# Two attention layers: column totals of two groups moved from TensorE to VectorE, and two chunks of statistics from VectorE to ScalarE

## The chip, the cores and the metric

The kernel runs on one core of one Trainium2 chip. The metric is device time in microseconds (us), lower is better; several runs are timed, and one further execution is recorded by the hardware profiler. The engines are called by the profile's letters: PE is TensorE (PEld its weight loads), DVE is VectorE, ACT is ScalarE, POOL is GpSimd, SP is SyncE, which here only issues transfers. Each engine works through its own instructions in order, and waits for the others by semaphores.

## The reference

The input `x` is eight images of 512 channels by 32x32 positions, all fp32. Two attention layers follow each other, each added to its input. Layer 0, which the change concerns, is cut here to what matters; `_gn` is a group norm over 16 channels and all positions:

```python
x = x + _L0_conv_ref(_gn(x), ...)          # layer 0
x = x + _L1_conv_ref(_gn(x), ...)          # layer 1

def _L0_conv_ref(x, gn_w, gn_b, qkv_w, qkv_b, proj_w, proj_b):
    normed = groupnorm(x) * gn_w + gn_b
    q, k, v = split(einsum('oc,bct->bot', qkv_w, normed) + qkv_b, 3)
    # 8 heads of 64 channels, 1024 positions each
    weight = softmax(einsum('bct,bcs->bts', q * scale, k * scale))   # over s
    a = einsum('bts,bcs->bct', weight, v)
    return einsum('oc,bct->bot', proj_w, xf + a) + proj_b
```

So per image and head, layer 0 needs the exponentials of 1024x1024 scores, their sums over one axis (the softmax denominators), the weighted values, and a division. Layer 1 begins with the group norm of layer 0's result, for which each channel's mean and variance over its 1024 positions are needed.

## The kernel before

**Stages.** Layer 0 runs image after image ("batch" `b`, 0 to 7); after all of them layer 1 does the same. In a batch, `attention0(b, ag)` computes the attention of layer 0; then the projections `qk0` and `v0` of the next batch, and `out0(b)`, the output projection of this one, which adds into the tiles `xs[b][c]` (four chunks of 128 channels by 1024 positions) and stores them to device memory (line 1080). At the last batch the projections of layer 1's first image stand in the place of the next batch's.

**The attention.** It goes over 64 steps `i`. Eight steps make a group `g` (two heads, 512 query positions, eight blocks of 128 key positions). A step has: four matmuls of scores into a PSUM tile `s` (line 1102; two such tiles), one ScalarE exponential of 128x1024 into a tile `e` (line 1107; seven such tiles, pool `epool`), one VectorE addition of `e` into the group's accumulator `zacc` (lines 1115 and 1117), and four matmuls of values (line 1130). When a group is complete, ScalarE copies its result out of PSUM to `u` (line 1141), and three jobs follow: `totals(g)` sums `zacc` over its partitions, `reciprocals(g)` inverts the sums and sends them through device memory so that they come back broadcast over partitions in `rzb`, and `finish(g)` multiplies `u` by `rzb` and adds it to `xa` (lines 1203 and 1205).

`totals` has two forms. For odd groups TensorE multiplies `zacc` by ones (line 1149), ScalarE copies the row out of PSUM (line 1154), and one transfer on SP brings it to a column `zc`. For even groups VectorE transposes `zacc` in blocks of 32x32 and reduces along the rows, twice (lines 1162 and 1163), transposes the small result (line 1167), and four transfers on SP gather it; `reciprocals` then adds one reduce (line 1179).

**Order.** The order of instructions on all engines is the order in which the Python code issues them (`manual_schedule`). The loop takes two steps at a time: scores of `i` and `i+1`, then values and sums of `i-2` and `i-1`, then what an `Agenda` holds for the slots `i` and `i+1`. A group that ends at step `i-1` puts `totals` at slot `i+2`, `reciprocals` at `i+6` (TensorE form) or `i+8` (VectorE form), and `finish` at `i+12`. Work with fixed slots in the same agenda:

- `start_xa` (line 886), four ScalarE passes that begin the tile `xa`, at slots 2, 4, 6, 8;
- `stats_out(b - 1, c)`, the statistics of the previous batch's output chunk `c` by two `bn_stats` and one `bn_aggr` on VectorE (lines 664 and 665), at slots 4, 7, 12, 15, and one slot after each the load of the next batch's chunk into the tile that this frees;
- `stats0(b + 1)`: the next batch's norm, from slot 18 on. ScalarE makes two passes over each chunk (lines 838 and 844), VectorE a chain of small operations whose last part, `scale` (lines 812 to 825), stands at slot 49; two tiny matmuls stand between;
- `normalize0(b + 1, c)` (line 880), ScalarE's normalisation of the next batch, at slots 51, 54, 57, 60;
- in batches 0 to 2, four VectorE operations that combine weights, at slots 13, 14, 16, 17 (lines 784 to 790).

After the loop, `combine_right` (lines 899 to 902) forms four operands `tmp` from the normalised tile on VectorE, in the buffers of `e`. TensorE's first two products of the next projection need only the normalised tile, the third needs the second of these operands (line 900).

Of the kernel before, what the change touches and what calls it, by code (L numbers as in the profile page):

```python
# [9 lines left out]
F32 = mybir.dt.float32  # L10
I32 = mybir.dt.int32
AF = mybir.ActivationFunctionType
# [6 lines left out]
P = 128  # L19
# [448 lines left out]
def tile_two_attention_layers(  # L468
# [19 lines left out]
    nc = tc.nc  # L488
# [224 lines left out]
    with ExitStack() as l0:  # L713
# [168 lines left out]
        def start_xa(b, c):  # L882
            if c == 0:
                xa_t[b] = act.tile([P, NCC, T], F32, tag="xa", name=f"xa_{b}")
            gs = st0[b]
            nc.scalar.activation(
                xa_t[b][:, c], xs[b][c], AF.Identity,
                bias=gs.nb[:, c : c + 1], scale=gs.r1[:, c : c + 1],
            )
# [194 lines left out]
        def stats_out(b, c):  # L1084
            channel_stats(stat, xs[b][c], mvs[:, b, c], f"o0_{b}_{c}")

        NG = NT
        NI = NFB * (H // 2) * NG

        def attention0(b, agenda):  # L1090
# [51 lines left out]

            def totals(g):

                if g % 2:
                    HB = FB // 2
                    z = ps_a.tile([P, FB], F32, tag="a0", name=f"z_{b}_{g}", bufs=2)[:, :HB]
                    for c in range(4):
                        nc.tensor.matmul(
                            z[c * 32 : c * 32 + 32], ones[:, :32], zacc[g][:, c // 2, ts(c % 2, HB)],  # L1150
                            start=True, stop=True, tile_position=(0, c * 32),
                        )
                    row = zpool.tile([P, HB], F32, tag="row", name=f"row0_{b}_{g}", bufs=1)
                    nc.scalar.copy(row, z)
                    zc[g] = stat.tile([P, T // P], F32, tag="zc", name=f"zc_{b}_{g}")
                    nc.sync.dma_start(out=zc[g], in_=row[0::32])
                    return
                HN = FB // 32
                pz = stat.tile([P, 2, HN], F32, tag="pz", name=f"pz_{b}_{g}")
                for m in range(2):  # L1160
                    zt = zpool.tile([P, FB], F32, tag="zt", name=f"zt_{b}_{g}_{m}", bufs=1)
                    nc.vector.transpose(zt, zacc[g][:, m])
                    nc.vector.reduce_sum(
                        pz[:, m], zt.rearrange("p (n i) -> p n i", i=32), axis=AX.X
                    )
                pt = stat.tile([P, 32], F32, tag="pt", name=f"pt_{b}_{g}")
                nc.vector.transpose(pt, pz.rearrange("p m n -> p (m n)"))
                zc[g] = stat.tile([32, 4, 32], F32, tag="zc4", name=f"zc_{b}_{g}")
                for c in range(4):
                    nc.sync.dma_start(out=zc[g][:, c], in_=pt[c * 32 : c * 32 + 32])  # L1170

            def reciprocals(g):

                nc.vector.tensor_add(u[g][0], u[g][0], u[g][1])
                R, W = (P, T // P) if g % 2 else (32, 32)
                zs = zc[g]
                if g % 2 == 0:
                    zs = stat.tile([32, 32], F32, tag="zs0", name=f"zs_{b}_{g}")
                    nc.vector.reduce_sum(zs, zc[g].rearrange("p c j -> p j c"), axis=AX.X)
                rz = stat.tile([P, 32], F32, tag="rz0", name=f"rz_{b}_{g}")[:R, :W]  # L1180
                nc.vector.reciprocal(rz, zs)
                zd = dram.tile([2, FB], F32, tag=f"zd0_{b}_{g}", name=f"zd0_{b}_{g}")
                nc.sync.dma_start(
                    out=zd if g % 2 else zd.rearrange("m (n j) -> (m n) j", j=32), in_=rz
                )
                rzb[g] = zpool.tile([P, FB], F32, tag="rzb", name=f"rzb_{b}_{g}")
                for m in range(2):
                    nc.sync.dma_start(
                        out=rzb[g][m * D : m * D + D], in_=zd[m].partition_broadcast(D)
                    )  # L1190
                col = b * H + g
                junk = stat.tile([P, 32], F32, tag="junk0", name=f"junkz_{b}_{g}")[:R, :W]
                nc.vector.tensor_scalar(
                    junk, zs, 1.0, 0.0, ALU.mult, ALU.add, accum_out=chk[:R, 1, col : col + 1]
                )
                nc.vector.scalar_tensor_tensor(
                    junk, rz, 1.0 / RZ_MAX, rz, ALU.mult, ALU.mult,
                    accum_out=chk[:R, 0, col : col + 1],
                )
# [5 lines left out]
                nc.vector.tensor_add(dst, dst, u[g][0])  # L1205


            for i in range(0, NI + 2, 2):
                if i < NI:
                    scores(i)  # L1210
                    scores(i + 1)
                if i >= 2:
                    for w in (i - 2, i - 1):
                        values(w)
                        sums(w)
                    if (i - 1) % NG == NG - 1:
                        g = (i - 1) // NG
                        agenda.at(i + 2, lambda g=g: totals(g))
                        agenda.at(i + 6 + 2 * (g % 2 == 0), lambda g=g: reciprocals(g))
                        agenda.at(i + 12, lambda g=g: finish(g))  # L1220
                agenda.run(i)
                agenda.run(i + 1)
# [19 lines left out]
        for b in range(B):  # L1242
# [1 line left out]
            ag = Agenda()  # L1244
            ag.at(1, lambda: bias_xa(b))
            for c in range(NCC):
                ag.at(2 + 2 * c, lambda c=c: start_xa(b, c))
            for c, slot in enumerate((4, 7, 12, 15)):
                if b > 0:
                    ag.at(slot, lambda c=c: stats_out(b - 1, c))  # L1250
                if more:
                    ag.at(slot + 1, lambda c=c: load_x(b + 1, c))
# [4 lines left out]
                for i, slot in enumerate((13, 14, 16, 17, 19)):  # L1257
                    ag.at(slot, lambda which=which, i=i: combine_left(which, [i]))
            if more:
                stats0(b + 1, ag, 18)  # L1260
                for c in range(NCC):
                    ag.at(51 + 3 * c, lambda c=c: normalize0(b + 1, c))
                ag.at(32, lambda: load_left("k", b + 1))
                ag.at(33, lambda: load_left("v", b + 1))
            else:

                def load_first():
                    t = n_t["1"] = shared.tile([P, NCC, T], F32, tag="n", name="y_0")
                    for c in range(NCC):
                        nc.sync.dma_start(out=t[:, c], in_=x1_d[0][ts(c, P), :])  # L1270

                ag.at(20, load_first)
                for slot, fn in zip((22, 25, 28), group_stages(0, B - 1, small_psum)):
                    ag.at(slot, fn)
                ag.at(32, lambda: load_left("q1", 0))
                ag.at(33, lambda: load_left("k1", 0))
                for c in range(NCC):
                    ag.at(49 + 4 * c, lambda c=c: normalize_to(n_t["1"][:, c], 0, c))
# [905 lines left out]
```

## Time and profile before

| What | Value |
|---|---|
| Median of 3 runs | 3907.03 us (3902.49 to 3908.03) |
| The profiled execution | 3899.99 us, its span 3898.1 us |
| Granted TensorE clock | 0.999 |
| TensorE matmul calls of totals (line 1149) | 32 calls, 256 records, 20.4 us busy |
| VectorE transposes and reduces of totals (lines 1162 and 1163) | 64 and 64, 708 and 686 ns each |
| VectorE statistics of the output (line 664) | 64, 680 ns each |
| ScalarE passes of the next batch's norm (lines 838 and 844) | 28 and 28, 1067 and 1156 ns each |

How to read the lines of the profile. A line of a group gives line number, engine, operation, the tile written, an arrow and the tiles read, shapes, how many, then busy time and the mean length of one in nanoseconds, then the time that the engine stood idle just before them and what it waited for. A timeline line gives start and length in us, the engine, the line number and the operation; lengths of merged rows can overlap the next start, since operations are pipelined, so the cost of one is read from start to start. The stretches give the busy time of each engine within each piece of the span. A matmul in fp32 appears as two records.

### The profile page before, as it was taken

How to read it: one execution, taken by the hardware profiler on the slowest of the kernel's cores; microseconds unless marked ns; L12 is line 12 of the kernel's file. 1: busy time of each engine (PE TensorE's matmuls, PEld its weight loads, DVE VectorE, ACT ScalarE, POOL GpSimd, SP SyncE). 2: the span in 40 equal slices, each digit the busy share in tenths (PEclk: the TensorE clock that was granted, in tenths of full speed). 3: DMA queues.
4: the chain of work that ended last, by engine and by line, in shares of the span. 5: the costliest groups of instructions: out<-in, count | busy, mean ns of one | idle time of the engine just before them, and what ended most of it. 6: DMA issues, size and time to landing. Idle time of an engine off the chain costs nothing. (4 is left out here: it accounts for less than half of the span.)

```text
span 3898.1 us, 95183 instructions
## 1 busy us (share of the span) xinstructions
PE 3845.0 (99%) x41612; PEld 1809.6 (46%) x41612; DVE 2840.8 (73%) x3921; ACT 1962.0 (50%) x2400; POOL 207.4 (5%) x210
## 2 busy tenths in 40 slices
PE   8999999999999999999999999999999999999999
PEld 4353535344353535344554544545545545445455
DVE  4858586675859485866967958859769668678598
ACT  1726354453627172534826717528438257176175
POOL 0000000000000000000110200201101102002000
PEclk9999999999999999999999999999999999999999
DMA  3313131111122121216947929749659479297385
GB/s 122 123 52 118 50 113 43 67 67 71 58 73 67 59 81 49 91 47 162 235 133 194 231 91 232 194 127 240 180 136 239 150 171 237 96 222 206 119 222 161
DMA packets 248440, 519.45 MB, mean 133 GB/s; under 512 B 49872, under 2 KB 57040, under 8 KB 241360
## 3 DMA queue, kind: packets, MB, share of 16 engines
q1 hardware_dynamic: 240832, 500.48, 45.3%
q0 software_dynamic: 7184, 12.81, 1.6%
q8 instruction: 328, 5.37, 0.6%
q14 instruction: 96, 0.79, 0.1%
HBM read 197.16 MB, written 46.92 MB: 63 GB/s over the span
## 5 line engine op out<-in xcount | busy, mean ns | idle before, releaser
L1766 DVE STREAM_TRANSPOSE et<-e 128x2048 f32<-128x2048 f32 x256 | 590.0, 2305 | 190.4 <-ACT e L1751 189.3
L1796 PEld LDWEIGHTS a<-et,v 128*64 128x64 f32 x16384 | 505.7, 138 | 283.8 <-issue 266.1
L1780 DVE BATCH_NORM_STATS2 bn<-e 128x6 f32<-128x512 f32 x1024 | 635.7, 683 | 0.0
L1107 ACT ACTIVATE e<-s 128x1024 f32<-128x1024 f32 x512 | 496.9, 1024 | 233.0 <-PE s L1102 233.0
L1713 ACT COPY raw<-s 128x1024 f32<-128x1024 f32 x480 | 470.1, 1018 | 224.8 <-PE s L1701 201.3
L1751 ACT ACTIVATE e<-m 128x1024 f32<-128x1024 f32 x512 | 496.2, 1021 | 165.7 <-issue 62.4
L1796 PE MATMUL a<-et,v 128*64 128x64 f32 x16384 | 553.3, 224 | 0.0
L1701 PE MATMUL s<-k,q 64*64 64x512 f32 x4096 | 513.2, 605 | 2.7 <-DVE v L1060 1.4
L1102 PE MATMUL s<-q,k 64*64 64x512 f32 x4096 | 490.4, 594 | 2.3 <-ACT e L1107 2.3
L1117 DVE TENSOR_TENSOR zacc<-zacc,e 128x1024 f32<-128x1024 f32 x384 | 467.5, 1217 | 27.2 <-ACT e L1107 1.4
L1130 PE MATMUL a<-e,v 64*64 64x512 f32 x4096 | 484.1, 589 | 0.0
L1738 PE MATMUL m<-re,wmix 32*32 32x512 f32 x8192 | 306.2, 599 | 14.8 <-DMA re<-raw 11.8
L1130 PEld LDWEIGHTS a<-e,v 64*64 64x64 f32 x4096 | 156.7, 133 | 282.8 <-issue 282.5
L1102 PEld LDWEIGHTS s<-q,k 64*64 64x64 f32 x4096 | 146.2, 133 | 284.4 <-issue 220.2
L1844 POOL DMA_DIRECT2D zd<-rz x96 | 52.5, 552 | 3361.9 <-DMA y<-x 1846.6
L1701 PEld LDWEIGHTS s<-k,q 64*64 64x64 f32 x4096 | 127.2, 132 | 216.0 <-issue 95.5
L1812 ACT COPY q<-a 64x256 f32<-64x256 f32 x256 | 94.0, 367 | 138.7 <-PE a L1796 137.1
L1738 PEld LDWEIGHTS m<-re,wmix 32*32 32x32 f32 x8192 | 68.1, 103 | 154.3 <-ACT raw L1713 65.9
L1509 PE MATMUL pv_t<-wv,y 128*128 128x512 f32 x256 | 120.6, 609 | 0.0
L920 PE MATMUL pv_p<-left_v,tmp 128*128 128x256 f32 x512 | 113.1, 379 | 0.0
L920 PE MATMUL pk_p<-tmp,left_k 128*128 128x512 f32 x256 | 112.5, 592 | 0.0
L920 PE MATMUL pq_p<-tmp,left_q 128*128 128x512 f32 x256 | 112.5, 592 | 0.0
(332 smaller groups left out, 3918.3 us busy)
## 6 DMA issues: line engine op xcount, KB each, us to landing
re<-raw SPq DMA_DIRECT2D x1024, 256.0 KB
left_q<-left_q SPq DMA_DIRECT2D x17, 1792.0 KB
left_p<-left_p SPq DMA_DIRECT2D x17, 1792.0 KB
left_k<-left_k SPq DMA_DIRECT2D x10, 1792.0 KB
x<-in_x_dram SPq DMA_DIRECT2D x32, 512.0 KB
rzb<-zd SPq DMA_DIRECT2D x128, 128.0 KB
x<-x SPq DMA_DIRECT2D x64, 256.0 KB
y<-x SPq DMA_DIRECT2D x32, 512.0 KB
```

Source lines behind the costliest of these rows:

```text
L920: nc.tensor.matmul(out, st, mv, start=start, stop=(k == 1), skip_group_check=True)
L1102: nc.tensor.matmul(ps[c * D : c * D + D, m], k[r, hp, k0 : k0 + D], q[r, hp, ts(f, FB)], start=True, stop=True,)
L1107: nc.scalar.activation(e[i], ps, AF.Exp, scale=S0 * S0)
L1117: nc.vector.tensor_add(zacc[g], zacc[g], e[i])
L1130: nc.tensor.matmul(acc[g][a][m * D : m * D + D], v[rows, kc, ts(2 * hp + m, D)], e[i][rows, m], start=(kc == 0), stop=(kc == NG - 1),)
L1701: nc.tensor.matmul(ps[c * D : c * D + D, m], qo_t[b][r, p, hp, ts(c, D)], k_t[b][r, hp, ts(kh, FB)], start=True, stop=True,)
L1713: nc.scalar.copy(dst, ps)
L1738: nc.tensor.matmul(ps[a // 2][c * 32 : c * 32 + 32, a % 2].rearrange("p (r h k) -> p h r k", r=2, h=2), wmix[rows].rearrange("p g i -> p ( ...
L1751: nc.scalar.activation(e[:, :, 2 * h : 2 * h + 2].rearrange("p r a k -> p a r k"), ps[h].rearrange("p a (r k) -> p a r k", r=2), AF.Exp,)
L1766: nc.vector.transpose(self.et[p, u].rearrange("p kb (r st a) g q -> p st kb r (a g q)", r=2, st=2)[:, st], self.e[p, s].rearrange("p r a ( ...
L1780: nc.vector.bn_stats(self.bn[n][:, p % 2, s, a], e[:, :, a].rearrange("p r k -> p k r"))
L1796: nc.tensor.matmul(acc[two * D : two * D + D, s].rearrange("p (x q) -> p x q", q=4), v_t[b][:, kb, ts(g, D)], et[:, kb, :, g], start=(kb = ...
```

## The change

Groups are told apart by `by_tensor(g)`, true for `g % 4 == 3`: groups 3 and 7 keep the TensorE form of `totals`, and groups 1 and 5 take the VectorE form, with its later slot for `reciprocals`. In batches 1 to 7, the statistics of the previous output's chunks 0 and 1 are made by ScalarE: a pass with a running sum, and, with the mean subtracted, a pass of squares, both writing over the chunk itself (nothing reads it any more); VectorE scales the two sums to mean and variance. `start_xa` moves to slots 6, 16, 28 and 40, the loads of the next batch's first two chunks to slots 10 and 12, and the next batch's norm by two slots.

```diff
+        def stats_out_pair(b, agenda):
+            sums = stat.tile([P, 2, 2], F32, tag="osum", name=f"osum_{b}")
+            neg = stat.tile([P, 2], F32, tag="oneg", name=f"oneg_{b}")
+            def first(c):
+                x = xs[b][c]
+                nc.scalar.activation(x, x, AF.Identity, accum_out=sums[:, 0, c : c + 1])
+            def second(c):
+                x = xs[b][c]
+                nc.scalar.activation(
+                    x, x, AF.Square, bias=neg[:, c : c + 1], accum_out=sums[:, 1, c : c + 1]
+                )
+            def moments(m):
+                if m == 0:
+                    nc.vector.tensor_scalar_mul(neg, sums[:, 0], -1.0 / T)
+                nc.vector.tensor_scalar_mul(mvs[:, b, :2, m], sums[:, m], 1.0 / T)
+            for c in range(2):
+                agenda.at(2 + 2 * c, lambda c=c: first(c))
+                agenda.at(9 + 2 * c, lambda c=c: second(c))
+            agenda.at(6, lambda: moments(0))
+            agenda.at(13, lambda: moments(1))
...
-                if g % 2:
+                if by_tensor(g):
...
+            def by_tensor(g):
+                return g % 4 == 3
...
-                        agenda.at(i + 6 + 2 * (g % 2 == 0), lambda g=g: reciprocals(g))
+                        agenda.at(i + 6 + 2 * (not by_tensor(g)), lambda g=g: reciprocals(g))
...
-                ag.at(2 + 2 * c, lambda c=c: start_xa(b, c))
-            for c, slot in enumerate((4, 7, 12, 15)):
-                if b > 0:
+                ag.at((6, 16, 28, 40)[c], lambda c=c: start_xa(b, c))
+            if b > 0:
+                stats_out_pair(b - 1, ag)
+            for c, slot in enumerate((9, 11, 12, 15)):
+                if b > 0 and c >= 2:
                     ag.at(slot, lambda c=c: stats_out(b - 1, c))
                 if more:
                     ag.at(slot + 1, lambda c=c: load_x(b + 1, c))
...
-                stats0(b + 1, ag, 18)
+                stats0(b + 1, ag, 20)
                 for c in range(NCC):
-                    ag.at(51 + 3 * c, lambda c=c: normalize0(b + 1, c))
+                    ag.at(53 + 3 * c, lambda c=c: normalize0(b + 1, c))
```

## The prediction

> **What bounds the kernel now.** I read the page first, then stretches of 14 us through one batch of layer 0, then VectorE's and TensorE's timelines through that batch. The page:
>
> ```profile
> span 3898.1 us, 95183 instructions
> PE 3845.0 (99%) x41612; PEld 1809.6 (46%) x41612; DVE 2840.8 (73%) x3921; ACT 1962.0 (50%) x2400; POOL 207.4 (5%) x210
> L1117 DVE TENSOR_TENSOR zacc<-zacc,e 128x1024 f32<-128x1024 f32 x384 | 467.5, 1217 | 27.2 <-ACT e L1107 1.4
> ```
>
> TensorE is the bound: 99%, and the longest of its waits is at the start. VectorE's 73% looks like room. It is an average; in the attention of batch 5 (1152 to 1266 us) the stretches say otherwise:
>
> ```profile
> core 0: us, PE busy (x) PEld busy (x) DVE busy (x) ACT busy (x) POOL busy (x), PEclk, DMA share, GB/s
> 1222.00:1236.00 14.00, 14.00 (x128) 4.99 (x124) 13.13 (x24) 8.83 (x10) 0.00 (x0) 1.00 0.10 23
> 1236.00:1250.00 14.00, 14.00 (x136) 4.80 (x132) 13.00 (x34) 10.52 (x13) 0.00 (x0) 1.00 0.06 20
> 1250.00:1264.00 14.00, 14.00 (x136) 4.82 (x132) 13.38 (x22) 11.83 (x13) 0.00 (x0) 1.00 0.09 21
> ```
>
> VectorE works 13.0 to 13.4 of 14 us there. The timelines of the same batch's last microseconds show how close it runs. VectorE, then TensorE:
>
> ```profile
> start us, us, engine line op out<-in xcount [idle before <-releaser]
> 1269.19 0.18 DVE L1196 SCALAR_TENSOR_TENSOR junkz<-rz 32x32 f32<-32x32 f32 x1
> 1269.31 1.21 DVE L899 TENSOR_TENSOR tmp<-n 128x1024 f32<-128x1024 f32 x1
> 1270.62 1.23 DVE L900 TENSOR_TENSOR tmp<-n,tmp 128x1024 f32<-128x1024 f32 x1
> ```
>
> ```profile
> 1264.73 1.04 PE L1130 MATMUL a<-e,v 64*64 64x512 f32 x8
> 1265.70 7.13 PE L920 MATMUL pk_p<-n,left_k 128*128 128x512 f32 x16
> 1272.67 1.88 PE L920 MATMUL pk_p<-tmp,left_k 128*128 128x512 f32 x4
> ```
>
> VectorE ends the attention at 1269.31 and makes the operands of the next projection; the second (L900) is ready at 1271.85. TensorE does the products that need none of them, and takes up that operand at 1272.67: 0.82 us to spare. The same reading of batches 0 to 7 gives 1.33, 0.33, 1.27, 1.10, 1.37, 0.82, 1.17, 1.07: 8.5 us together. Whatever makes VectorE later than that by the end of an attention, TensorE waits for.
>
> **The change, part by part.** Groups 1 and 5 of each of the 8 batches go from TensorE to VectorE.
>
> *TensorE loses* 16 calls. One, in batch 2:
>
> ```profile
> 547.07 1.90 PE L1102 MATMUL s<-q,k 64*64 64x512 f32 x16
> 548.79 1.90 PE L1130 MATMUL a<-e,v 64*64 64x512 f32 x16
> 550.61 0.64 PE L1149 MATMUL z<-zacc,ones 128*32 128x256 f32 x8
> 551.18 1.95 PE L1102 MATMUL s<-q,k 64*64 64x512 f32 x16
> 554.67 1.90 PE L1102 MATMUL s<-q,k 64*64 64x512 f32 x16
> ```
>
> Two pairs of scores take 6.87 us without it (two periods of 3.434) and 7.60 with it: 0.73 us a call, 11.7 us over 16. It counts only if TensorE still sets the end.
>
> *VectorE gains*, per group, the totals and the longer reciprocal. In batch 5 the totals run from 1168.67 to 1171.74 (two transposes, two reduces, a small transpose): 3.07 us. The reciprocal part takes 1.54 us (1181.88 to 1183.42) where that of a TensorE group takes 0.97 (1193.57 to 1194.54). Together 3.64 a group, 7.28 a batch, 58.2 over eight. Rate by rate: a TensorE group costs VectorE 7 sums at 1.21, 0.97 and 1.33 for the finish, 10.8 us; a VectorE group 14.4, and TensorE passes a group in four pairs, 13.7. Two kinds in turn average 12.6, under 13.7; three of four the dear kind, and with the norm's small operations on top, it is over.
>
> *VectorE loses* two chunks of statistics in seven batches, 1.44 us each (1158.68 to 1160.12). This buys nothing. They stood at slots 4 and 7; VectorE then waits for the exponentials of slot 10 all the same (start at 1167.53 after 1.05 us idle), and the two chunks left, at 12 and 15, stood there before. What is taken out ahead of that wait only lengthens it. Behind it the second pass adds a scaling of 0.08 us, 0.6 in all.
>
> *What VectorE's idle time takes in.* Between slot 10 and L899 the timelines of the batches hold 28.6 us of VectorE's waits above 0.15 us. Later work swallows those where the other side is on time: the broadcast of group 0 (in batch 5: 2.49), single waits for exponentials and for ScalarE's first passes. That is 3.08, 0.70, 0.17, 2.79, 2.70, 2.80, 2.70, 1.99 by batch: 16.9. Not swallowed are the broadcast of group 2, which follows VectorE's own reciprocal by the same few operations as before (1.52 in batch 5, 9.4 in all), and group 3's total, queued on SP behind that broadcast (2.3 in all).
>
> *Sum.* VectorE reaches L899 later by 58.2 + 0.6 - 16.9 = 41.9; less the 8.5 to spare, TensorE's next projection starts 33.4 us later over the eight batches, from 3 in batch 0 to 6 in batches 1 and 2, whose weight combinations fill VectorE already. The 11.7 us are inside this: TensorE only waits longer. Both ends: all waits swallowed, 58.8 - 28.6 - 8.5 = +21.7; none, +50.3. I take +33.4, since each wait was judged by what it waits for.
>
> [...] In the rows, the reduce of 128x512 takes 686 ns and an addition of that size 684. [...]
>
> *ScalarE gains* 28 passes, rows of 1067 and 1156 ns plus 0.2 for the accumulator, and loses 16 row copies of 375 ns. Between pairs of exponentials it idles about 1.5 us (1172.41 to 1175.90), and each pass has a pair of its own in the place of a start_xa; the one behind the copies of group 0 replaces a start_xa there. Cost 0; if a first pass had to wait for the store of its chunk (issued by 1152, pass at 1157), it would be up to 1 us in 14 places, under VectorE's lag anyway. Worked in place, nothing in these rows gives another duration.
>
> *SP.* The load of chunk 0 now waits for a ScalarE pass that ends near 1170.2; behind it stand group 0's small copies, ready at 1171.7, so nothing is held. Chunk 1 (about 1175.5) holds chunks 2 and 3, which wait for VectorE at 12 and 15 as before. The passes that read the loads start two slots later. Cost 0; the lengthened group 0 broadcast has 3.07 us of cover.
>
> *The norm, two slots later.* Its scale now follows group 5's totals on VectorE, some 5 us later than now (1243.77 in batch 5), and ScalarE's first normalisation holds the next exponentials about 4 us. TensorE has one score tile in hand and 1.5 us of ScalarE's idle time; it would lose about 2 to 3 us there, against 0.73 per removed call gained. That is less than VectorE's lag at the end, so it moves a part of the wait forward and adds nothing.
>
> **Rivals.**
> - *The lag is absorbed, faster.* Seven exponential tiles are 12 us of TensorE's pace (7 by 1.717), less an exponential and a sum (2.2): VectorE can lag 8 to 10 us before ScalarE stops. If it caught up by the projection, all 11.7 us would stand: 3895. For it: 73% over the span. Against it: 13.4 of 14 in the stretch. It decides at (28.6 + 8.5) / 8 = 4.6 us of added work a batch; the rows say 7.3. [...]
> - *The new groups wait for their broadcasts too.* If each of the 16 waited as group 2 does now (9.4 us over 8, 1.17 each), 18.7 more: 3959. Against it: behind a VectorE group the next totals lie between reciprocal and finish, some 7.1 us, and the broadcast took 5.7 to 6.6 in batch 5.
> - *ScalarE becomes the bound by the late norm alone.* If VectorE's lag at the end is less than summed, TensorE still loses 3 us a batch there against 1.46 gained: +12, 3919. For it: ScalarE stands behind VectorE's scale even now (normalisation at 1243.80, scale ready at 1243.77).
> - *The move does nothing at all* (the totals hidden on both engines): 3907. Against it: the instructions move by the diff's own test, and neither engine has the room.
>
> **How the numbers follow.** The profiled execution took 3900.0 us, 7 under the median of 3907.0 and below the lowest of three (3902.5); the shift is put on the median: 3907.0 + 33.4 = 3940. Chances: my forecast (+21.7 to +50.3) 0.76, broadcasts 0.07, the late norm 0.10, nothing 0.02, absorbed 0.05. The ends 3929 and 3957 leave out more than 2 in 10, so the low one reaches on towards the late norm's case: 3923 to 3957. About 0.2% (7.8 us) is what a measurement can tell from no change: faster 0.05, same 0.02, slower 0.93.
>
> **What would show it.** Matmul records of z x128 instead of x256; zt and pz x96; VectorE idle under 3 us between slot 10 and L899, which comes some 5 us later against its batch's start; TensorE waiting for tmp (L900) and, on ScalarE's exponentials, for nn (L825), about 45 us together, so that its busy time falls by 10 while the span grows. I am wrong if TensorE's waits for tmp and for exponentials stay near zero, or if VectorE idles as long as now, by the broadcasts.

## The result, and the profile after

The changed kernel takes 3944.16 us (median of 5 runs, 3941.08 to 3945.94) against 3907.03 us for the kernel before (5 runs, 3902.49 to 3908.03): a ratio of 1.0097, 95% interval 1.0087 to 1.0108. It is slower by 37 us; the forecast was 3940, 33 slower. The profiled execution took 3944.32 us, its span 3942.6.

In the changed kernel's file the lines of the attention that are shown here stand 26 lower (L1107 is now L1133, L1117 is L1143, L1149 is L1175, L1196 is L1222); L899, L900 and L920 keep their numbers. From the page of the changed kernel, the span, the engines' busy time, and VectorE's largest group in layer 0:

```profile
span 3942.6 us, 95110 instructions
PE 3848.9 (98%) x41484; PEld 1806.9 (46%) x41484; DVE 2878.1 (73%) x3996; ACT 1984.0 (50%) x2440; POOL 207.4 (5%) x210
L1143 DVE TENSOR_TENSOR zacc<-zacc,e 128x1024 f32<-128x1024 f32 x384 | 467.8, 1218 | 39.8 <-ACT e L1133 13.9
```

TensorE has 128 instructions fewer (the 16 removed calls are 128 matmul records), VectorE works 37 us more, and its share of the span still reads 73%. One addition costs what it did (1218 ns). The page alone does not show why the span is 44.5 us longer. The stretches of the same part of batch 5 as before, counted from that batch's start, do (columns: stretch, its length, then busy time and records of each engine, granted clock, DMA):

```profile
core 0: us, PE busy (x) PEld busy (x) DVE busy (x) ACT busy (x) POOL busy (x), PEclk, DMA share, GB/s
1248.00:1262.00 14.00, 14.00 (x134) 4.96 (x130) 12.99 (x25) 9.58 (x12) 0.00 (x0) 1.00 0.08 22
1262.00:1276.00 14.00, 12.65 (x118) 4.31 (x110) 13.00 (x36) 8.07 (x10) 0.00 (x0) 1.00 0.07 21
1276.00:1290.00 14.00, 13.55 (x128) 4.54 (x132) 13.41 (x21) 12.19 (x15) 0.00 (x0) 1.00 0.06 21
```

VectorE is as full as it was, and now TensorE is not: it stands idle for 1.35 and 0.45 us in stretches where it had 14.00 of 14. At the end of the same attention, VectorE's timeline and then TensorE's:

```profile
start us, us, engine line op out<-in xcount [idle before <-releaser]
1299.08 0.18 DVE L1222 SCALAR_TENSOR_TENSOR junkz<-rz 32x32 f32<-32x32 f32 x1
...
1299.19 1.21 DVE L899 TENSOR_TENSOR tmp<-n 128x1024 f32<-128x1024 f32 x1
1300.54 1.22 DVE L900 TENSOR_TENSOR tmp<-n,tmp 128x1024 f32<-128x1024 f32 x1
```

```profile
1288.68 3.61 PE L1156 MATMUL a<-e,v 64*64 64x512 f32 x32
1292.22 7.29 PE L920 MATMUL pk_p<-n,left_k 128*128 128x512 f32 x16
1301.81 8.42 PE L920 MATMUL pk_p<-tmp,left_k 128*128 128x512 f32 x19 [2.30 <-DVE tmp L900]
```

Before, the operand of L900 lay ready for 0.82 us when TensorE came to it. Now TensorE has done its two products (7.29 us) and waits 2.30 us, and starts 0.05 us after the operand is there; those 0.05 us are the same in all eight batches. The chain of cause reads upward: operand late, because L899 is 118.53 us behind the batch's first addition where it was 114.42, because VectorE did two more groups' totals.

TensorE's waits in layer 0 (90 to 1745 us of the span; columns: waiting engine and line, what it waited for, us in total, times, longest):

```profile
engine line waited for: us in total, times, longest us
PE s L1128 <- ACT e L1133: 19.0, 17, 4.2
PE pk_p L920 <- DVE tmp L900: 11.7, 7, 2.3
PE pq_p L920 <- DVE tmp_y L900: 2.3, 1, 2.3
```

Before (90 to 1700 us), the other two were not there, and the first was:

```profile
PE s L1102 <- ACT e L1107: 2.3, 8, 0.3
```

The wait for exponentials is VectorE's lag too, passed on earlier in the batch: the next batch's scale (VectorE) is late, the normalisation behind it holds ScalarE, and the exponentials queue behind that. The longest is in batch 1: VectorE ends the scale at 410.55, ScalarE has waited 6.03 us for it, and TensorE 4.23 us when the next exponentials are done.

Batch by batch, from a batch's first addition on VectorE: how much later TensorE takes up the operand of L900, as forecast (7.28 + 0.08, less the idle time and the spare time listed in the prediction) and as measured, and how much longer the batch is to the start of the next (the last one: to that same product).

| Batch | 0 | 1 | 2 | 3 | 4 | 5 | 6 | 7 | Sum |
|---|---|---|---|---|---|---|---|---|---|
| operand, forecast | 2.9 | 6.3 | 5.9 | 3.5 | 3.3 | 3.7 | 3.5 | 4.3 | 33.4 |
| operand, measured | 3.5 | 7.0 | 5.3 | 2.9 | 3.9 | 3.4 | 3.5 | 4.3 | 33.7 |
| batch, measured | 3.6 | 7.1 | 7.1 | 3.0 | 4.0 | 3.5 | 3.6 | 4.3 | 36.2 |

Layer 1 is the same code in both kernels. From that last product to the end it took 2201.7 us in the profiled execution of before and 2208.9 in that of after; in the twelve experiments' profiles it was 2203.1 to 2223.9. The spans differ by 44.5 us: 36.2 in the batches, 7.2 in layer 1, 1.1 ahead of the first batch; layer 1's part lies within that spread.

### The profile page after: what moved, and what is told of

Same layout as the page of the kernel before. It is cut to its first block, busy times and chain, and to the rows that moved or that the text cites. A ratio compares the mean times of both kernels' runs of the same rounds, so it can differ in the third digit from the quotient of the medians.

```text
span 3942.6 us, 95110 instructions
## 1 busy us (share of the span) xinstructions
PE 3848.9 (98%) x41484; PEld 1806.9 (46%) x41484; DVE 2878.1 (73%) x3996; ACT 1984.0 (50%) x2440; POOL 207.4 (5%) x210
## 5 line engine op out<-in xcount | busy, mean ns | idle before, releaser
L1133 ACT ACTIVATE e<-s 128x1024 f32<-128x1024 f32 x512 | 497.4, 1026 | 213.4 <-PE s L1128 213.1
L1143 DVE TENSOR_TENSOR zacc<-zacc,e 128x1024 f32<-128x1024 f32 x384 | 467.8, 1218 | 39.8 <-ACT e L1133 13.9
L920 PE MATMUL pk_p<-tmp,left_k 128*128 128x512 f32 x256 | 114.9, 602 | 11.7 <-DVE tmp L900 11.7
L920 PE MATMUL pv_p<-left_v,tmp 128*128 128x256 f32 x512 | 113.1, 379 | 0.0
L920 PE MATMUL pq_p<-tmp,left_q 128*128 128x512 f32 x256 | 112.5, 592 | 0.0
```

The lines of the kernel that those rows point to most:

```text
L920: nc.tensor.matmul(out, st, mv, start=start, stop=(k == 1), skip_group_check=True)
L1133: nc.scalar.activation(e[i], ps, AF.Exp, scale=S0 * S0)
L1143: nc.vector.tensor_add(zacc[g], zacc[g], e[i])
```

## The experiments

My theory: VectorE's lag at the end of each attention is the whole loss, and its only source is the totals of the two groups. Rivals: the late norm or the passes on ScalarE cost something by themselves; the new groups wait for their broadcasts. Where nothing else is said, a diff is against the changed kernel; "before" in the measured times is the kernel before, on the same chip. "Operand" and "batches" are the sums of the table above, always against the profile of before.

### One part alone

The totals alone, in the kernel before:

```diff
-                if g % 2:
+                if by_tensor(g):
...
+            def by_tensor(g):
+                return g % 4 == 3
...
-                        agenda.at(i + 6 + 2 * (g % 2 == 0), lambda g=g: reciprocals(g))
+                        agenda.at(i + 6 + 2 * (not by_tensor(g)), lambda g=g: reciprocals(g))
```

> The kernel before, with groups 1 and 5 moved to VectorE and nothing else: statistics, start_xa, loads and the norm at their old places. Theory (VectorE's work behind slot 10 decides; the chunks of statistics taken out ahead of it bring nothing): as the whole change, +33 to +40 us against before, and VectorE reaches the operand of line 900 about 5 us later against its batch's start. Rival (the late norm or ScalarE's passes cause a good part of the loss): clearly less, +10 to +25.

Measured: 3944.14 us, ratio 1.0104 (1.0087 to 1.0121), +40.3 us; operand +33.4, batches +39.3. The batches exceed the operand's delay by 5.8 us, 1.8 in each of batches 0 to 2; behind TensorE's wait at the end of each of these three the profile shows 3.41 us at half the granted clock, a matter taken up with the chunks below.

The rest alone, in the changed kernel (statistics on ScalarE, loads, norm and start_xa at the new slots, four groups on each engine):

```diff
             def by_tensor(g):
-                return g % 4 == 3
+                return g % 2 == 1
```

> The whole change except that groups 1 and 5 stay on TensorE: statistics of chunks 0 and 1 on ScalarE, start_xa spread, norm two slots later. Theory: VectorE has nothing more to do behind slot 10, so within 3 us of before, and TensorE does not wait for line 900 more than now. Rival (ScalarE's passes in place and the late norm cost time by themselves): +10 us or more, with TensorE waiting for exponentials.

Measured: 3902.92 us, ratio 0.9995 (0.9986 to 1.0005); operand +0.2, batches +0.3. The moved statistics cost nothing and buy nothing, and the whole loss is in the totals. Why they buy nothing shows in VectorE's timeline of batch 5 at the exponentials of slot 10, in the kernel before and then in the changed one:

```profile
1167.53 1.23 DVE L1115 TENSOR_TENSOR zacc<-e,e 128x1024 f32<-128x1024 f32 x1 [1.05 <-ACT e L1107]
```

```profile
1188.91 2.55 DVE L1143 TENSOR_TENSOR zacc<-zacc,e 128x1024 f32<-128x1024 f32 x2 [0.73 <-ACT e L1133]
1193.32 1.23 DVE L1141 TENSOR_TENSOR zacc<-e,e 128x1024 f32<-128x1024 f32 x1 [1.85 <-ACT e L1133]
1194.46 0.70 DVE L1188 STREAM_TRANSPOSE zt<-zacc 128x512 f32<-128x512 f32 x1
```

With two chunks of statistics taken from it, VectorE waits 1.85 us there, where it waited 1.05 (and more at the additions ahead of it), and that addition starts 12.65 us behind the batch's first one in both kernels. The chunks stood ahead of the place where VectorE is short of time, and time saved ahead of a wait goes into the wait.

### The norm at its old slots

```diff
-                stats0(b + 1, ag, 20)
+                stats0(b + 1, ag, 18)
...
-                    ag.at(53 + 3 * c, lambda c=c: normalize0(b + 1, c))
+                    ag.at(51 + 3 * c, lambda c=c: normalize0(b + 1, c))
```

> The whole change, with the next batch's norm back at its old slots (18, normalisations from 51). Theory: the late norm only moves a part of TensorE's wait forward, so within 4 us of the changed kernel (+33 to +41 against before): the waits for exponentials shrink from 19 us and those for the operand of line 900 grow from 14 by as much. Rival (the late norm is a cost of its own): 10 to 20 us better than the changed kernel.

Measured: 3948.43 us, ratio 1.0106 (1.0089 to 1.0122); operand +31.8, batches +36.0. The time lies a little above what was expected (+33 to +41), but the batches are as long as the changed kernel's (+36.2); layer 1, whose code is the same, takes 4.8 us longer in the profiled execution. TensorE's wait for exponentials falls from 19.0 to 11.8 us in layer 0, and its wait for the operand of L900 rises from 11.7 to 15.6 (and that for ScalarE's operand of L944 from 0.2 to 4.1). The late norm moves the wait within the batch and is not a cost of its own.

### How many groups: one more, or three more, than before

```diff
-                return g % 4 == 3
+                return g in (3, 5, 7)
```

> The whole change, but of the two groups only group 1 goes to VectorE; group 5 stays on TensorE. Theory (a threshold: VectorE has some 2 us of idle time behind slot 10 and 1 us to spare at the end of a batch, and 3.7 us are added): nearly all swallowed in batches 0 and 3 to 7, some 2 us lost in each of batches 1 and 2: +2 to +8 us against before, far under half of +37. Rival (each moved group costs its share): half of the loss, about +18.

Measured: 3917.40 us, ratio 1.0031 (1.0018 to 1.0043), +13.5 us; operand +4.2, batches +4.7. Only batches 1, 2 and 7, which have the least idle and spare time, are longer (2.6, 1.9 and 2.4); the others are shorter by 0.2 to 0.7, since there the 3.64 us of added work are no more than about what idle and spare time hold together (3.6 to 4.4). Layer 0 did what the theory says; the time did not, and was between the two expectations. The profiled execution, at 3924.3 us 7 above the median, spent 2220.4 us in layer 1, whose code is unchanged, and has four stretches of half clock there (they come up with the chunks, below). Why this kernel draws more of that than others is not settled.

```diff
-                return g % 4 == 3
+                return g == 7
```

> The whole change, with group 3 on VectorE too (seven of eight). Theory: 3.64 us more a batch, 29 us, of which VectorE's idle time at the broadcast of group 2 and at group 3's total (13.4 us together in the changed kernel) takes in most: +16 on the changed kernel, about +53 us against before. Rival (each moved group costs the same 37/16 us): +55. What tells: VectorE's waits for the broadcast of group 2 vanish.

Measured: 3959.07 us, ratio 1.0143 (1.0123 to 1.0162), +56 us; operand +46.7, batches +47.4. The time does not tell the expectation (+53) from the rival (+55); the waits do. VectorE's wait for the broadcast of group 2 ahead of L899 is gone. In the changed kernel, too, group 2's broadcast is the only one that VectorE waits for there (10.5 us in eight waits), and none of the 16 moved groups waits for its own. So a VectorE group gives its own broadcast enough cover, and the rival that new groups would wait for theirs falls. Layer 0 of this kernel also has 44 us at half clock, but the operand is late by what VectorE is: L899 comes 54.5 us later over the eight batches, less 8.5 to spare.

### The other two chunks on ScalarE

If time saved ahead of the wait at slot 10 is worth nothing, time saved behind it should be worth its full length. Here ScalarE takes chunks 2 and 3, which VectorE would do at slots 12 and 15, and VectorE keeps 0 and 1:

```diff
-            for c in range(2):
-                agenda.at(2 + 2 * c, lambda c=c: first(c))
-                agenda.at(9 + 2 * c, lambda c=c: second(c))
+            for c in (2, 3):
+                agenda.at(2 * c - 2, lambda c=c: first(c))
+                agenda.at(2 * c + 5, lambda c=c: second(c))
...
-            for c, slot in enumerate((9, 11, 12, 15)):
-                if b > 0 and c >= 2:
+            for c, slot in enumerate((4, 7, 12, 15)):
+                if b > 0 and c < 2:
```

> The whole change, but ScalarE takes the statistics of chunks 2 and 3, which stood at slots 12 and 15, and VectorE keeps those of chunks 0 and 1 at slots 4 and 7 (loads at 5, 8, 13, 16 as in the kernel before). The same amount of work moves, but now from behind slot 10. Theory: VectorE reaches line 900's operand 2 times 1.44 us earlier in seven batches, 20 us together, so the loss falls from +37 to about +17 us. Rival (only the amount moved counts, not its place): as the changed kernel, +37.

Measured: 3936.84 us, ratio 1.0080 (1.0059 to 1.0100), +33.9 us. The operand is later by 17.0, just the +17 expected, and yet the batches are longer by 27.7. The difference, 11 us, is a new term. It shows in TensorE's timeline and in the stretches around it (batch 5 of this kernel; PEclk is the granted clock):

```profile
1286.04 7.27 PE L920 MATMUL pk_p<-n,left_k 128*128 128x512 f32 x16
1295.62 6.68 PE L920 MATMUL pk_p<-tmp,left_k 128*128 128x512 f32 x11 [2.31 <-DVE tmp L900]
```

```profile
core 0: us, PE busy (x) PEld busy (x) DVE busy (x) ACT busy (x) POOL busy (x), PEclk, DMA share, GB/s
1292.00:1296.00 4.00, 1.69 (x5) 0.53 (x4) 3.80 (x10) 1.00 (x2) 0.00 (x0) 1.00 0.07 25
1296.00:1300.00 4.00, 4.00 (x7) 1.52 (x6) 1.83 (x2) 0.00 (x0) 0.00 (x0) 0.57 0.11 42
1300.00:1304.00 4.00, 4.00 (x11) 1.85 (x10) 1.22 (x1) 0.00 (x0) 0.00 (x0) 1.00 0.00 0
```

Directly behind the wait TensorE does 7 matmuls in 4 us instead of 11, at a mean granted clock of 0.57. The trace's records of the clock say 0.5 from 1296.00 for 3.41 us. In this execution it happens in six of the first seven batches, each some 1.8 us longer than its operand's delay. In the changed kernel it costs that only in batch 2 (7.1 against 5.3 in the table); of the other stretches of its layer 0, three lie in attentions at whose end TensorE waits for the operand all the same, and one behind the last product.

### Is it TensorE's idleness that brings the half clock?

The same kernel, but TensorE fills the wait with three products that nothing reads, so its work grows:

```diff
+        fill_at = {f"pk0_{b}" for b in range(1, B)} | {"pq1_0"}
...
+            if nm in fill_at:
+                z = small_psum(f"{nm}_fill")
+                for w in (FB, FB, FB // 2):
+                    nc.tensor.matmul(
+                        z[:, :w], left[:, 0, 0, :P], b11[:, 0, :w], start=True, stop=True
+                    )
```

> As the kernel with chunks 2 and 3 on ScalarE (+33.9 us against the kernel before, of which the later first product with tmp explains 16.9), but TensorE does three products whose result nothing reads, about 2.15 us, between the second and the third product of the next projection, the place where it stood idle for 2.3 us in seven batches. VectorE's and ScalarE's work is unchanged. Theory that an idle TensorE of about 2 us brings a stretch at half clock behind it: the granted clock stays at 1 behind each projection of layer 0, and about 1.75 us in seven batches (11 to 12 us) is won back, so +20 to +24 against before, although TensorE has more to do. Rival that the 17 us beyond the shift come from the waits themselves or from VectorE: the time stays at +32 to +36, or grows where the added products come on top.

Measured: 3931.20 us, ratio 1.0069 (1.0053 to 1.0084), +23.5 us against the median of before; operand +20.0, batches +20.6. TensorE's timeline of batch 5 (its L921 is L920 elsewhere):

```profile
1279.95 7.29 PE L921 MATMUL pk_p<-n,left_k 128*128 128x512 f32 x16
1287.08 2.31 PE L951 MATMUL pk_fill<-n,left_k 128*128 128x512 f32 x6
1289.55 10.57 PE L921 MATMUL pk_p<-tmp,left_k 128*128 128x512 f32 x24 [0.16 <-DVE tmp L901]
```

The 24 records with `tmp` take 10.57 us; in batch 2 of the changed kernel, at half clock, 17 took 9.26. One stretch of half clock is left in layer 0 (at 410.5 us, behind a wait for exponentials), instead of seven, and the batches exceed the operand's delay by 0.6 us, no longer by 11. (The stretch that is left lies in batch 1, where TensorE comes to the operand 1.22 us after it is ready and the operand's own delay is 5.3 us, in place of 2.8 without the filling.) So in these two kernels the half clock went with TensorE standing idle (2.31 us ahead of the operand in batch 5 without the filling, 0.16 with it), not with the late operand. In the medians the gain is less certain, since the two intervals overlap; the profiled execution without the filling took 3951.6 us, its median is 3936.8.

### Sums on GpSimd

GpSimd is busy for 5% of the span. It takes the addition of the two halves of `u`, 684 ns on VectorE in each group:

```diff
-                nc.vector.tensor_add(u[g][0], u[g][0], u[g][1])
+                nc.gpsimd.tensor_add(u[g][0], u[g][0], u[g][1])
```

> The whole change, with the first addition of reciprocals (u0 + u1) on GpSimd, which does nothing in layer 0. It takes 0.60 us, start to start, from VectorE in each of seven groups ahead of line 899: 4.2 us a batch. Theory: the loss of some 4.6 us a batch nearly vanishes, 2 to 3 us being left in each of batches 1 and 2: between -3 and +10 us against before. Rival (the exponentials' chain through the late norm, or the broadcasts, hold TensorE as well): +12 or more stays. Were VectorE slowed by GpSimd's reading beside it, its additions would take longer than 1.22 us.

Measured: 3935.86 us, ratio 1.0076 (1.0056 to 1.0096), +33 us; operand +27.9, batches +28.6. That is the side of the rival (+12 or more), mostly because VectorE's additions took longer beside one on GpSimd, the sign that the last sentence of the expectation names: 1525 ns in the mean, not 1217. Between slot 10 and L899, 34.3 us are taken from VectorE over the eight batches (56 additions at 0.61, start to start), but its other operations there take 26.6 us longer, so that 7.7 are left, and 5.8 arrive at the operand. The timeline of batch 1 shows VectorE's additions with a GpSimd addition beside them, that of batch 4 a small operation:

```profile
352.13 3.44 DVE L1143 TENSOR_TENSOR zacc<-zacc,e 128x1024 f32<-128x1024 f32 x2
...
353.02 1.48 POOL L1200 TENSOR_TENSOR u<-u,u 128x512 f32<-128x512 f32 x1 [12.06 <-ACT u L1167]
```

```profile
1019.91 1.28 POOL L1200 TENSOR_TENSOR u<-u,u 128x512 f32<-128x512 f32 x1 [11.62 <-ACT u L1167]
...
1019.97 1.27 DVE L1222 SCALAR_TENSOR_TENSOR junkz<-rz 32x32 f32<-32x32 f32 x1
```

Two additions take 3.44 us; elsewhere in that batch two take 2.51. Over layer 0, 58 of the 448 additions into `zacc` overlap one on GpSimd by more than 0.2 us and take 1525 ns in the mean (longest 2306), the other 390 take 1217: 18 us given back. Another 7.0 are in L1222, 0.18 us long in the changed kernel and here up to 1.27, as long as the GpSimd addition beside it. So the move helped little, and no run here shows why VectorE's operations get longer beside GpSimd's. GpSimd itself took 1.3 to 2.4 us for one.

The gain is uneven because what is given back is: 1.4 to 2.3 us of 4.3 in batches 0, 3, 5 and 6, which are longer than before by only 0.3 to 1.0; all of it in batches 1 and 4, and 6.3 us in batch 2. Batches 1 and 2, 9.3 and 8.3 us longer than before, are even longer than in the changed kernel (7.1 each). There the rival's other part shows as well: TensorE waits 5.4 and 3.6 us for exponentials behind the late norm, half clock follows both waits, and in batch 1 the operand lies ready for 1.28 us when TensorE comes to it.

Chunks 2 and 3 on ScalarE, the norm early, and the addition on GpSimd, together:

```diff
-            for c in range(2):
+            for c in (2, 3):
...
-                nc.vector.tensor_add(u[g][0], u[g][0], u[g][1])
+                nc.gpsimd.tensor_add(u[g][0], u[g][0], u[g][1])
...
-                stats0(b + 1, ag, 20)
+                stats0(b + 1, ag, 18)
```

> The two before together, with the norm at its old slots: six of eight groups on VectorE, chunks 2 and 3 on ScalarE, the addition on GpSimd. VectorE's work behind slot 10 is then 7.3 - 2.9 - 4.2 = 0.2 us a batch above that of the kernel before. Theory: TensorE no longer waits, and the 16 removed calls show, 0.73 us each: -6 to -12 us against before. Rival (the calls lay beside other work and cost nothing): within 3 us of before.

Measured: 3928.96 us, ratio 1.0062 (1.0043 to 1.0081), +26 us; operand +23.8, batches +24.5. The miss has the same cause in the main: against chunks 2 and 3 alone, VectorE's work between slot 10 and L899 is only 2.5 us shorter, of the 34.3 taken from it. Of the 31.8 given back 17 are additions into `zacc` (45 overlap one on GpSimd by more than 0.2 us and take 1583 ns), the rest small operations. VectorE's idle time there is 9 us longer besides.

### VectorE relieved where it is short of time

If VectorE's lag is the loss, VectorE's own work can be cut where it is short, without GpSimd. The first form: chunks 2 and 3 on ScalarE, the norm at its old slots, the reciprocals of group 6 behind `combine_right`, and the two small operations by which the kernel keeps watch on each VectorE group's sums (L1219 and L1222 of the changed kernel) done once a batch over all six:

```diff
+            agenda.at(90, check_all)
...
-                    zs = stat.tile([32, 32], F32, tag="zs0", name=f"zs_{b}_{g}")
+                    zs = kept[0][:, n]
...
+                if n is None:
+                    check(zs, rz, R, W, b * H + g)
...
-                        agenda.at(i + 6 + 2 * (not by_tensor(g)), lambda g=g: reciprocals(g))
+                        agenda.at(i + 6 + 2 * (not by_tensor(g)) + 1.5 * (g == 6), lambda g=g: reciprocals(g))
...
                 combine_right(f"{b + 1}", n_t[b + 1])
+                ag.run(65.5)
```

> Six groups on VectorE as in the change, with VectorE's own work per batch cut in three places: ScalarE takes the output's chunks 2 and 3 (ahead of the slots where VectorE is full) instead of 0 and 1, 2.9 us; the reciprocals of group 6 stand behind the combination of the next projection's operands instead of ahead of it, 1.5 us; the two check operations of each of the six groups are done once a batch over all six after the attention, about 2.2 us. The next batch's norm is at its old slots. Nothing of the result is left out. Theory that VectorE's lag at the end of each attention is the whole loss: the change put 7.3 us a batch on VectorE and 33.4 us of it arrived; with 6.6 a batch taken off (53 us) TensorE waits for no operand (L900) any more and keeps the 11.7 us of the removed totals, less what ScalarE's passes cost: -12 to 0 us against the kernel before. Rival that the loss has another part (TensorE's waits for exponentials, SP's order, the clock): +10 or more remains though the operand is there in time.

Measured: 3911.71 us, ratio 1.0013 (1.0004 to 1.0023), +4 to +5 us; operand +0.9, batches +1.6. The loss is all but gone, as the theory says, but the gain that it forecast (-12 to 0) is not there: TensorE still waits for the operand in all eight batches, 0.57 us in one and 0.75 in seven. The second form moves the totals of group 6 behind `combine_right` too:

```diff
-                        agenda.at(i + 2, lambda g=g: totals(g))
+                        agenda.at(65.5 if g == 6 else i + 2, lambda g=g: totals(g))
...
-                        agenda.at(i + 12, lambda g=g: finish(g))
+                        agenda.at(75 if g == 6 else i + 12, lambda g=g: finish(g))
```

> As the kernel with the three cuts (+1.3 per mille, layer 0 by batch 211.0 to 212.5 us against 211.5), where the operand of L900 was still late by 0.8 us in seven batches, but the totals of group 6 too (3.07 us of VectorE) stand behind the combination of the next projection's operands. Nothing of the result is left out. If VectorE's lag at that place is the rest of the loss, the 0.8 us vanish, and the batches fall to 210.1 to 210.9 us (210.07 is the batch before less two removed totals of 0.73 us), so -6 to -11 us in layer 0; layer 1, which varies by some 10 us between executions, adds its spread, so -11 to 0 us in the time. Rival that TensorE's cycle without the removed calls has another floor (its waits for exponentials, the evacuations that are now later): 211.0 us a batch or more, and a time of 0 to +10.

Measured: 3903.02 us, ratio 0.9987 (0.9978 to 0.9996), -2.7 us; operand -7.5, batches -6.5. Batches 1 to 3 and 5 take 210.2 to 210.4 us where the kernel before takes 211.5, near the 210.07 that two calls of 0.73 less would give; batches 0, 4 and 6 take 211.3 to 211.7, and in 0 and 6 TensorE still waits 0.75 us for the operand. In the medians the gain is 0.1%, and the profiled execution, in which the batches are 6.5 us shorter, took 3908.0 us, 5 above the median, with 2215.0 of them in layer 1. VectorE's timeline of batch 5, then TensorE's:

```profile
1265.59 1.22 DVE L899 TENSOR_TENSOR tmp<-n 128x1024 f32<-128x1024 f32 x1
1266.91 1.23 DVE L900 TENSOR_TENSOR tmp<-n,tmp 128x1024 f32<-128x1024 f32 x1
...
1270.33 0.70 DVE L1195 STREAM_TRANSPOSE zt<-zacc 128x512 f32<-128x512 f32 x1
```

```profile
1262.20 7.13 PE L920 MATMUL pk_p<-n,left_k 128*128 128x512 f32 x16
1269.17 10.46 PE L920 MATMUL pk_p<-tmp,left_k 128*128 128x512 f32 x24
```

The operand is ready at 1268.14, 1.03 us before TensorE comes to it, and the totals run beside the projection. Batch 5 is the best of the seven with a next batch; in the others the operand is ready 0.05 to 0.66 us ahead. The control is the same form with four groups on each engine:

```diff
-                return g % 4 == 3
+                return g % 2 == 1
```

> The control for the kernel with group 6 behind the combination: the same cuts of VectorE's work, but the totals of groups 1 and 5 stay on TensorE as in the kernel before (four groups each). If TensorE bounds that form, cutting VectorE's work buys nothing: batches of 211.5 us as before, -3 to +3 us in the time. Rival that the cuts by themselves shorten or lengthen the kernel (the order at the end of the attention, ScalarE's passes): another batch time than 211.5 by over 0.3 us, and the difference between the two forms is then not the price of the two groups alone.

Measured: 3911.51 us, ratio 1.0013 (1.0004 to 1.0022); operand -0.9, batches +0.8, and 4.32 us or more to spare at the operand, which buy nothing. Beside this control the two groups' move is worth 3911.51 - 3903.02 = 8.5 us of the 11.7 (7.3 in the batches of the two profiles): the idea of the change pays once VectorE has the room for it. The control itself missed its range (-3 to +3): it is slower than before by 5.8 us, of which its batches show 0.8, 0.5 in batch 0 and 0.8 in batch 2 less 0.7 in batch 7; the rest isn't located, and the two lean forms too are 2 to 4 us dearer than their batches say. So, against the kernel before, only 2.7 of the 8.5 us are won.

| Kernel | Operand, us | Batches, us | Time against before, us | Ratio |
|---|---|---|---|---|
| the change | +33.7 | +36.2 | +37.1 | 1.0097 |
| totals alone | +33.4 | +39.3 | +40.3 | 1.0104 |
| the rest alone | +0.2 | +0.3 | -1.0 | 0.9995 |
| norm early | +31.8 | +36.0 | +44.6 | 1.0106 |
| five VectorE groups | +4.2 | +4.7 | +13.5 | 1.0031 |
| seven VectorE groups | +46.7 | +47.4 | +56.2 | 1.0143 |
| chunks 2 and 3 | +17.0 | +27.7 | +33.9 | 1.0080 |
| chunks 2 and 3, filled | +20.0 | +20.6 | +23.5 | 1.0069 |
| addition on GpSimd | +27.9 | +28.6 | +32.9 | 1.0076 |
| both | +23.8 | +24.5 | +26.0 | 1.0062 |
| lean | +0.9 | +1.6 | +4.0 | 1.0013 |
| leaner | -7.5 | -6.5 | -2.7 | 0.9987 |
| leaner, four groups | -0.9 | +0.8 | +5.8 | 1.0013 |

## Why the prediction was right, point by point

- *The sum.* Forecast: the operand later by 33.4 us over eight batches, the same sum on the time. Measured: 33.7 at the operand, 36.2 over the batches, 37.1 in the medians. Single batches were off by up to 0.7 either way, so the closeness of the sum is partly luck; the next two points show where.
- *VectorE gains 7.28 a batch; the moved statistics buy nothing.* Right in kind: the totals alone give 33.4 at the operand, the rest alone 0.2, and extra idle time appears at slot 10, as said. The size was a little high: between slot 10 and L899 VectorE's work rose by 55.3 us over the eight batches, not by 58.8. Most of the difference is at the addition ahead of the totals, which takes 1.14 us from start to start where a transpose follows and 1.31 where an addition does; the 3.07 us of the totals were counted in full on top of it.
- *Idle time swallowed.* Of 28.6 us (waits above 0.15 us) 14.8 are left, so 13.8 were swallowed, not 16.9. What was left was put at 9.4 (broadcast of group 2) and 2.3 (total of group 3) and is 10.5 and 3.0, with 1.4 us of other waits besides. Judging each wait by what it waits for held in kind; the two errors, 3.5 us of work and 3.1 us of waits, cancel, and L899 is later by 41.5 where 41.9 was forecast. That closeness is luck.
- *Spare time of 8.5 us used up first.* Right: 0.05 us is left in each batch.
- *The 11.7 us of TensorE count only if TensorE sets the end.* Right: they don't show until VectorE is relieved, and then 8.5 of them do beside the control.
- *The late norm adds nothing; ScalarE and SP cost nothing.* Right, by the norm's own experiment and by the statistics alone.
- *The low rival, the lag absorbed from 4.6 us a batch.* With one group (3.64 a batch) five batches absorb it and three don't. An average over batches was too coarse there: batches 1, 2 and 7 decide alone.
- *The rate of the totals.* Right: the four large operations of a group's totals take 2.8 us before and after (708 and 704 ns a transpose, 686 a reduce), and the reduce is no dearer than an addition of its size (684). From the rows of the additions, 684 ns for 128x512 and 1217 for 128x1024, I estimate 533 ns for 512 elements and some 150 for each instruction.
- *Left out: the half clock behind TensorE's waits.* The prediction priced a wait at its own length. In the changed kernel the missing term is 1.8 us in batch 2, with the totals alone 5.4, and with chunks 2 and 3 it was 11 us.
- *Wrong among the signs: TensorE's busy time falls by 10.* It rose by 3.9 on the page. Ten are gone with the calls (20.4 to 10.2 us), and six stretches of 3.41 us at half the clock lengthen what runs in them by 10.2; the rest of the rise I can't place, and the ends of matmuls are modelled. For the same reason the waits named in layer 0 are 33 us (19.0 + 11.7 + 2.3), and not 45.

## What to carry to other kernels

Before moving work to an engine with "27% free", read its busy share in the stretch where the work lands, and list the waits it has there with what each waits for: the sum of those that later work can swallow, and of the time that its results lie ready, is the room, batch by batch. Work taken off an engine counts only behind the last wait that it would have anyway; two chunks of statistics were worth 0 ahead of it and 17 us behind it. A new wait of 2.3 us on TensorE cost here up to 1.8 us more than its length (batch 2 of the changed kernel), so such a wait is worth filling or moving.

## What the runs showed of the hardware

*The half clock lay on a grid of 3.413 us.* The records of the granted clock begin at 23.3 us of the span in the kernel before and at 24.2 in the changed one; this holds from there up to 3880 us. In each profile, the stretches of granted clock 0.5 start at times that differ by whole multiples of 3.413 us, to within 0.01, and last 3.41 us or twice that. Cut into these cells, the spans of all fourteen profiles give TensorE's idle time in each. Every cell with over 2.0 us of it, 34 cells, was followed by half clock; of those with 1.82 to 2.0 nine were and six weren't; of those with less three were, besides the seven below. In the changed kernel the cells ahead of its six stretches hold 2.91, 2.31, 2.39, 1.99, 2.27 and 2.30 us, and the fullest one without half clock behind it 1.81; the kernel before has none over 1.76, and no half clock. So the same wait of 2.3 us cost 1.8 us more in batch 2 of the changed kernel, where it fell within one cell (idle 652.75 to 655.06, cell 652.23 to 655.64), and nothing more in batch 5, where it straddled two (idle 1299.51 to 1301.81, with an edge at 1300.77). In the kernel with chunks 2 and 3 the stretches repeat each 215.04 us, 63 cells: batch and grid had locked. Seven cells more, all where layer 1 begins (1797 to 1854 us), are at half clock though the profile shows no idle time in the cell ahead. In each cell ahead TensorE did products of eight columns, of which 128 stand together and take 3.9 to 4.7 us in all. In every profile these products lie across two cells: with 2.64 us or more of them in one cell (six profiles) half clock followed, with 2.53 or less (the other eight; 2.53 in the changed kernel) it did not. Idle time in the profile alone does not account for these seven.

*GpSimd beside VectorE.* An fp32 addition of 128x512 on GpSimd took 1.3 to 2.4 us, VectorE's additions of 128x1024 beside it 1525 ns in place of 1217, and a VectorE operation of 32x32 up to 1.27 us in place of 0.18.

*Executions differ in layer 1.* The same code took 2201.7 to 2223.9 us there, with TensorE's wait for the small transfers of `re` at 10.1 to 19.5 us and up to five half-clock stretches: the two longest, 2220.4 and 2223.9, have four and five, those with none take 2201.7 to 2208.0. Differences of under 5 us between kernels are not explained here.
